# Later GpSimd addends, later sums of h and later scales in a gated linear-attention block loop

## The chip, the cores and the metric

The kernel runs on one core of one Trainium2 chip. The metric is device time in microseconds (us): 1939.26 us is the median of three runs before the change (1938.48 to 1942.68). Engines are named as in the profile: PE is the matrix engine, PEld its weight loads, DVE is VectorE, ACT is ScalarE, POOL is GpSimd, SP is the queue that issues most DMAs.

## The reference, cut to what matters

All arrays are float32. src is 4 x 2048 x 256, there are 16 heads of 64, FF is 1024, and the gate's inner width I is 704.

```python
xn = layernorm(src)
# attention branch
Q, K, v = elu(xn @ Wq + bq) + 1, elu(xn @ Wk + bk) + 1, xn @ Wv + bv
o  = (Q @ (K^T v)) / (Q . sum(K) + 1e-6)          # per head
x1 = layernorm(xn + o @ Wo + bo) * g1 + be1
s  = layernorm(x1 + gelu(x1 @ W1 + b1) @ W2 + b2) * g2 + be2
# gate branch: x and h are rounded to a 4-bit grid in blocks of 16, and so are the weights
h = silu(fp4(xn) @ fp4(w_gate)^T) * (fp4(xn) @ fp4(w_up)^T)
g = silu(fp4(h) @ fp4(w_down)^T)
out = src + s * g
```

## The kernel before, in words

The 8192 rows are worked in 32 blocks of 256 rows (n = 0 to 31), 8 blocks to a batch. K^T v and the sum of K over a whole batch are needed before a block of that batch can be finished. So a first loop makes the keys of batch 0, and in the main loop (line 1041) the 24 blocks of batches 0 to 2 also make the keys of the batch after theirs, in two "subs" per block (each sub is 256 rows by half of the features). The 8 blocks of the last batch (n = 24 to 31) have no keys to make; `subs` is empty there.

A block of the main loop does, in the order of the program:

- `q_of` (741): the product pq, then Q on ACT and DVE, four pieces `zq<-e,q` (767);
- `keys_k` (511) for the first sub: product pk, `k<-pk,bk` (491), exp on ACT, `kk<-ek,k` on DVE (500), and on POOL the running sum `kacc` (502, 504);
- `quantized_x`, `quantized_h` (683, 689): the grid of x and h times its scales, `qT<-qT,gridT`. The scales reach qT by a DMA that spreads them (670), the grid by a transposing DMA (680). `sums` (769): pz, `z<-pz`, `z<-z`, and z goes out to memory and comes back spread as zb by DMAs;
- `gate_up` (694) of the next block: pg, and h by ACT and DVE; `keys_xk` (526): pxk from kk;
- `down` (719): pd, the gate g on ACT, then three POOL operations: `o = g*be2` (735), `o = o + src` (736), `g = g*g2` (737);
- `qz` (796): `zq<-zq,zb`, Q divided by its sum, in two halves on DVE;
- `ffn_sums` (861) for block n-1: four DVE operations `hs` on h^T, for a product with fewer multiplications (seven instead of eight);
- `keys_k` for the second sub; `attention` (802): pa, x1 = xn + pa, statistics, on POOL the power -0.5 (377), normalization; `keys_xk` for the second sub;
- most of `ffn_2(n-1)` (880): py; `scales_h(n+1, j)` for j = 0, 1 (642) and `scales_x(n+2)` (621): reduce, scale, reciprocal on DVE;
- `x1_T` (818): transposes of x1, then on POOL `x1*g1` (830) and `+ shift` (831);
- `grid_of_h`, `grid_of_x` (645, 625): the rounding to the grid, and after it on POOL `xn + bo` (640);
- `output(n-1)` (904): the sum of py and x1 (`s`), its statistics, on POOL the power -0.5, then `o<-s,rstd,o` and the store; `ffn_1(n)` (833): pf and hT.

What sets the order: every product keeps the order of the program on PE (98). DVE and ACT keep it in the first loop; from line 1026 on (`in_order[0] = False`) a scheduler fills them, which takes from the instructions that are ready, by its own estimate of times, the one that comes first in the program. POOL is filled in this way throughout. Each engine then executes its list strictly in order. `tc.issue_after(ins)` makes the instructions traced under it stand behind `ins` in their engine's list; it adds no wait on another engine. Products share four PSUM banks (`mm`), and q1, e and kk have three buffers each, xn, x1, g and o two, the tile x (src, loaded for line 736) one.

Of the kernel before, what the change touches and what calls it, by code (L numbers as in the profile page):

```python
# [12 lines left out]
ALU = mybir.AluOpType  # L13
# [9 lines left out]
def linear_attention_gated_by_fp4_ffn(  # L23
# [34 lines left out]
    nc = tc.nc  # L58
# [305 lines left out]
        yield  # L364


    def stats(x, name, js=range(TB)):

        j0, j1 = js[0], js[-1] + 1
        mv = small.tile([P, TB, 2], F32, tag="mv", name=f"mv_{name}")  # L370
        rstd = small.tile([P, TB], F32, tag="rstd", name=f"rstd_{name}")
        for j in js:
            st = small.tile([P, 6], F32, tag="st", name=f"st_{name}_{j}")
            vector.bn_stats(st, x[:, j, :])
            vector.bn_aggr(mv[:, j, :], st)
        vector.tensor_scalar(rstd[:, j0:j1], mv[:, j0:j1, 1], LN_EPS, None, ALU.add)
        nc.gpsimd.tensor_tensor(rstd[:, j0:j1], rstd[:, j0:j1], neg_half[:, j0:j1], ALU.pow)  # L377
        return mv, rstd

    def normalize(dst, x, mv, rstd):  # L380
# [115 lines left out]
    def key_elu(b, f, k1, e, nm, first):  # L496

        kacc = keys[b, "acc", f]
        kk = work.tile([P, HALF], F32, tag="kk", name=f"kk_{nm}", bufs=3)
        ins = vector.scalar_tensor_tensor(kk, e, 1.0, k1, ALU.min, ALU.max)  # L500
        if first:
            nc.gpsimd.tensor_copy(kacc, kk)
        else:
            nc.gpsimd.tensor_tensor(kacc, kacc, kk, ALU.add)  # L504
        return kk, ins.ins

    def key_xk(b, f, xn, j, kk, first, last):
# [105 lines left out]
    def load_xn(n):  # L613
        blk[n]["xn"] = work.tile([P, TB, D], F32, tag="xn", name=f"xn_{n}", bufs=2)
        nc.sync.dma_start(blk[n]["xn"], xn_d[n])

    def load_xnT(n):
        blk[n]["xnT"] = work.tile([P, ND, T], F32, tag="xnT", name=f"xnT_{n}", bufs=1)
        nc.sync.dma_start(blk[n]["xnT"], xnT_d[n])
# [5 lines left out]
    def grid_of_x(n, issue=None):  # L625
        xn = blk[n]["xn"]
        y = work.tile([P, TB * D // BLK, BLK], F32, tag="y", name=f"y_{n}", bufs=1)
        per_j = D // BLK
        out = [
            (  # L630
                grid_x[:, :, j, :].rearrange("p c (k e) -> p c k e", e=BLK),
                j * per_j, (j + 1) * per_j,
            )
            for j in range(TB)
        ]
        fp4_grid(
            blocks(xn.rearrange("p j d -> p (j d)")), blk[n].pop("rs_x"), y, out, f"x_{n}", issue
        )

        nc.gpsimd.tensor_tensor(xn, xn, rows["bo"], ALU.add)  # L640

    def scales_h(n, j):
        blk[n]["rs_h", j] = fp4_scale(blocks(blk[n]["h"][j]), scale[:, : I // BLK, j], f"h_{n}_{j}")
# [45 lines left out]
    def quantized_h(n, j):  # L689

        qh = qT[:, :NI, j * P : (j + 1) * P]
        return vector.tensor_tensor(qh, qh, gridT[n][:, j * NI : (j + 1) * NI, :], ALU.mult)
# [26 lines left out]
    def down(n, j):  # L719
        if j == 0:  # L720
            blk[n]["pd"] = acc_tile(f"pd_{n}").rearrange("p (j d) -> p j d", j=TB)
        pd = blk[n]["pd"]
        for i in range(NI):
            mm(
                pd[:, j, :], qT[:, i, j * P : (j + 1) * P], wd[:, i, :], start=i == 0, stop=i == NI - 1
            )
        if j < TB - 1:
            return
        g = work.tile([P, TB, D], F32, tag="g", name=f"g_{n}")
        scalar.activation(g, pd, AF.Silu)  # L730

        o = work.tile([P, TB, D], F32, tag="o", name=f"o_{n}")
        x = work.tile([P, TB, D], F32, tag="x", name=f"x_{n}", bufs=1)
        nc.sync.dma_start(x, rows_of(src, n))
        nc.gpsimd.tensor_tensor(o, g, rows["be2"], ALU.mult)  # L735
        nc.gpsimd.tensor_tensor(o, o, x, ALU.add)
        nc.gpsimd.tensor_tensor(g, g, rows["g2"], ALU.mult)
        blk[n]["g"], blk[n]["o"] = g, o


    def q_of(n, first=None):
# [54 lines left out]
    def qz(n):  # L796
        zq, zb = blk[n]["zq"], blk[n].pop("zb")
        for g in range(2):
            cs = slice(4 * g, 4 * g + 4)
            vector.tensor_tensor(zq[:, cs, :], zq[:, cs, :], zb[:, cs, :], ALU.mult)  # L800

    def attention(n):
        zq = blk[n].pop("zq")
# [14 lines left out]
    def x1_T(n):  # L818
        x1 = blk[n]["x1"]
        pt = transposes(x1, f"x1_{n}")  # L820
        x1T = work.tile([P, ND, T], F32, tag="x1T", name=f"x1T_{n}", bufs=1)
        for c in range(ND):
            ins = scalar.activation(
                x1T[:, c, :], pt[:, c, :], AF.Identity,
                bias=cols["be1"][:, c : c + 1], scale=cols["g1"][:, c : c + 1],
            )
        blk[n]["x1T"] = x1T
        blk[n]["act"] = ins.ins

        nc.gpsimd.tensor_tensor(x1, x1, rows["g1"], ALU.mult)  # L830
        nc.gpsimd.tensor_tensor(x1, x1, rows["shift"], ALU.add)

    def ffn_1(n, chunks=range(NF)):
        x1T = blk[n]["x1T"]
# [203 lines left out]


    last = NBLK - 1  # L1040
    for n in range(NBLK):
        b, bi = divmod(n, NB)
        subs = (2 * bi, 2 * bi + 1) if b + 1 < B else ()
        if n < last:
            gate = gate_up(n + 1)
        for sub in subs if n == 0 else ():
            keys_T(b + 1, sub)
        if subs:
            step(m_half)
            q_of(n)  # L1050
            step(down_1)
            load_xnT(n + 1)
            kk_ins = keys_k(b + 1, subs[0])
            with tc.issue_after(kk_ins):
                ins = quantized_x(n)
            with tc.issue_after(sums(n, ins.ins).ins):
                for j in range(TB):
                    quantized_h(n, j)
            if n > 0:
                keys_T(b + 1, subs[1], keys["exp"])  # L1060
            step(m_half)
            keys_xk(b + 1, subs[0])
            step(gate, 9)
            step(m_half)
            down(n, 0)
            down(n, 1)
        elif n < last:
            def values():
                quantized_h(n, 0)
                return quantized_x(n)  # L1070

            step(m_half)
            q_of(n, values)
            quantized_h(n, 1)
            load_xnT(n + 1)
            down(n, 0)
            sums(n)
            step(m_half)
            step(gate, 9)
            step(m_half)  # L1080
            down(n, 1)
        else:
            for j in range(TB):
                quantized_h(n, j)
                down(n, j)
        with tc.issue_after(blk[n + 1]["late"]) if n < last else nullcontext():
            qz(n)
        if not subs:
            ffn_2(n - 1, 4 if n < last else 8)
        if n > 0:  # L1090
            ffn_sums(n - 1)
        if subs:
            keys_k(b + 1, subs[1])
        attention(n)
        if n + 2 < NBLK:
            load_xn(n + 2)
        if subs:
            keys_xk(b + 1, subs[1])
            if subs[1] % NB == NB - 1:
                m_half = m_of_half(b + 1, subs[1] // NB)  # L1100
                step(m_half)
        bn, bin_ = divmod(n + 1, NB)
        next_subs = (2 * bin_, 2 * bin_ + 1) if bn + 1 < B else ()
        for sub in next_subs if n > 0 else ():
            keys_in(bn + 1, sub)
        if n > 0:
            ffn_2(n - 1, 20)
        more = n + 1 < NBLK, n + 2 < NBLK
        if more[0]:
            for j in range(TB):  # L1110
                scales_h(n + 1, j)
            if more[1]:
                scales_x(n + 2)
        for sub in next_subs if n == 0 else ():
            keys_in(bn + 1, sub)
        for sub in next_subs[:1]:
            keys_apart(bn + 1, sub)
        x1_T(n)
        for sub in next_subs[1:]:
            keys_apart(bn + 1, sub, blk[n]["act"])  # L1120

        if n > 0 and not subs:
            ffn_2(n - 1, 26)
        if more[0]:
            spread_scales(n + 1, *more)
        if n > 0:
            ffn_2(n - 1, 28)
        if more[0]:
            grid_of_h(n + 1, 0)
            grid_T(n + 1, 0, NI)  # L1130
            grid_of_h(n + 1, 1, blk[n]["act"])
            if more[1]:
                grid_of_x(n + 2, blk[n]["act"])
            grid_T(n + 1, NI, (NCH if more[1] else NI) * TB)
        if n > 0:
            output(n - 1)
        if n + 1 == last:
            q_of(last)
            ffn_1(n, range(NF // 2))
            sums(last)  # L1140
            ffn_1(n, range(NF // 2, NF))
        else:
            ffn_1(n)
        for sub in next_subs[:1]:
            keys_T(bn + 1, sub, blk[n]["gelu"])
# [38 lines left out]
```

## Time and profile before

| | |
|---|---|
| median of 3 runs | 1939.26 us |
| the profiled execution | 1948.53 us, span 1946.4 us, granted PE clock 0.995 |
| PE busy | 1895.5 us, 97% of the span, 8788 instructions |
| DVE busy | 1440.9 us, 74% |
| ACT busy | 803.7 us, 41% |
| POOL busy | 562.3 us, 29%, 461 instructions |
| mean DMA traffic | 96 GB/s |

POOL's operations that the change moves, each 32 times, by 128 x 512 elements, with the mean time of one:

| line | what | mean ns |
|---|---|---|
| 735 | o = g*be2 | 1567 |
| 736 | o = o + src | 1708 |
| 737 | g = g*g2 | 1867 |
| 830 | x1 = x1*g1 | 1274 |
| 831 | x1 = x1 + shift | 1418 |
| 640 | xn = xn + bo | 1402 |

How to read it: the times of the profile count from the start of the span. A row of the timeline gives the start, the busy time of the instructions that it merges (their number stands at the end, x2), the engine, the line, the operation, out<-in, and in brackets how long the engine was idle before it and what ended that. Nearly all DVE and ACT instructions have line 115, since a helper records them; they are told apart by their tiles. An fp32 product appears as two PE instructions for each one of the program. The end of a PE instruction is modelled: instructions of one kind start 0.216 us apart (128x256, 32 of them in 7.07 us) while each is shown as 0.38 us long.

### The profile page before, as it was taken

The numbers are of one execution on the slowest core, as the hardware profiler recorded it, in microseconds if no ns is written. First come the engines' busy times: TensorE is split into PE (matmuls) and PEld (weight loads), VectorE is DVE, ScalarE is ACT, GpSimd is POOL, SyncE is SP. The second block draws the span as 40 slices with busy tenths as digits, with TensorE's granted clock in tenths as the row PEclk, the third lists the DMA queues.
The fourth block names the chain that finished last, engine by engine and source line by source line (L and its number), as shares of the span: only waits on it lengthen the run. The fifth ranks groups of instructions, "written<-read, shape, count | busy, mean of one in ns | idle before, by whom it ended". The sixth has DMA issues, their size and how long they took to land. (4 is left out here: it accounts for less than half of the span.)

```text
span 1946.4 us, 24467 instructions
## 1 busy us (share of the span) xinstructions
PE 1895.5 (97%) x8788; PEld 1379.9 (71%) x8788; DVE 1440.9 (74%) x2554; ACT 803.7 (41%) x1384; POOL 562.3 (29%) x461
## 2 busy tenths in 40 slices
PE   9989999999999999999999999999999999999997
PEld 4446677667777777777677777776776688788776
DVE  7878577776677777777777778776767778788775
ACT  2334554334444355542344543444433344444342
POOL 4441233322233232332222333222323212222212
PEclk9999999999999999999999999999999999999999
DMA  4435545344444455644343553465442444445441
GB/s 148 146 93 119 114 102 108 101 102 86 87 70 94 113 101 118 134 80 101 84 85 71 118 109 101 97 122 104 84 90 65 71 81 86 82 90 89 76 80 42
DMA packets 225120, 187.11 MB, mean 96 GB/s; under 512 B 103364, under 2 KB 185568, under 8 KB 225000
## 3 DMA queue, kind: packets, MB, share of 16 engines
q1 hardware_dynamic: 224168, 183.99, 44.8%
q10 hardware_dynamic: 832, 1.57, 0.3%
q8 instruction: 69, 1.13, 0.3%
q14 instruction: 51, 0.42, 0.1%
HBM read 131.41 MB, written 31.54 MB: 84 GB/s over the span
## 5 line engine op out<-in xcount | busy, mean ns | idle before, releaser
L99 PE MATMUL pg<-wgu,qT 128*128 128x352 f32 x1024 | 310.4, 461 | 0.1
L99 PEld LDWEIGHTS pg<-wgu,qT 128*128 128x128 f32 x1024 | 193.2, 190 | 118.7 <-issue 14.0
L504 POOL TENSOR_TENSOR kacc<-kacc,kk 128x512 f32<-128x512 f32 x120 | 171.9, 1433 | 339.8 <-DVE kk L115 337.7
L99 PE MATMUL pxk<-kk,xn_k 128*128 128x512 f32 x512 | 237.1, 602 | 19.7 <-DVE kk L115 19.6
L99 PE MATMUL pa<-m,zq 128*128 128x256 f32 x1024 | 229.9, 382 | 8.2 <-DVE zq L115 8.0
L99 PE MATMUL pk<-wk_sb,xnT_k 128*128 128x512 f32 x512 | 232.1, 596 | 1.4 <-ACT xnT_k L115 1.0
L99 PE MATMUL pq<-xnT,wq_sb 128*128 128x256 f32 x1024 | 228.0, 381 | 1.6 <-ACT hT L115 1.6
L99 PEld LDWEIGHTS pa<-m,zq 128*128 128x128 f32 x1024 | 194.5, 191 | 47.6 <-issue 13.0
L99 PE MATMUL pf<-x1T,w_sb 128*128 128x256 f32 x1024 | 226.7, 379 | 0.0
L115 ACT ACT_TABLE_LOAD x122 | 156.5, 1283 | 166.8 <-DVE k L115 153.9
L99 PEld LDWEIGHTS pq<-xnT,wq_sb 128*128 128x128 f32 x1024 | 195.6, 191 | 28.8 <-ACT hT L115 2.0
L735 POOL TENSOR_TENSOR o<-g,be_r 128x512 f32<-128x512 f32 x32 | 50.1, 1567 | 573.5 <-ACT g L115 549.8
L99 PEld LDWEIGHTS pf<-x1T,w_sb 128*128 128x128 f32 x1024 | 192.0, 190 | 25.5 <-issue 0.4
L99 PEld LDWEIGHTS pxk<-kk,xn_k 128*128 128x128 f32 x512 | 91.5, 189 | 129.6 <-issue 78.0
L99 PE MATMUL pd<-wd,qT 128*128 128x256 f32 x768 | 172.4, 379 | 1.7 <-DVE qT L115 1.7
L99 PEld LDWEIGHTS pk<-wk_sb,xnT_k 128*128 128x128 f32 x512 | 97.6, 191 | 104.1 <-issue 97.4
L99 PEld LDWEIGHTS pd<-wd,qT 128*128 128x128 f32 x768 | 145.7, 190 | 26.2 <-DVE qT L115 2.7
L115 DVE SCALAR_TENSOR_TENSOR zq<-e,q 128x512 f32<-128x512 f32 x128 | 86.8, 688 | 104.2 <-ACT e L115 104.2
L377 POOL TENSOR_TENSOR rstd<-rstd,neg_half 128x2 f32<-128x2 f32 x96 | 72.8, 759 | 283.4 <-DVE rstd L115 266.2
L115 ACT ACTIVATE h<-pg 128x352 f32<-128x352 f32 x128 | 58.9, 460 | 191.5 <-PE pg L99 191.5
L115 ACT ACTIVATE ek<-k,neg_one 128x512 f32<-128x512 f32 x128 | 89.7, 719 | 116.3 <-DVE k L115 115.9
L115 DVE SCALAR_TENSOR_TENSOR kk<-ek,k 128x512 f32<-128x512 f32 x128 | 90.2, 713 | 61.6 <-ACT ek L115 61.6
(133 smaller groups left out, 2776.9 us busy)
## 6 DMA issues: line engine op xcount, KB each, us to landing
zb<-z_d SPq DMA_DIRECT2D x128, 256.0 KB
qT<-scale_d SPq DMA_DIRECT2D x248, 128.0 KB
x_k<-in_L_attn_src_dram SPq DMA_DIRECT2D x32, 256.0 KB
x<-in_L_attn_src_dram SPq DMA_DIRECT2D x32, 256.0 KB
xn_d<-xn_k SPq DMA_DIRECT2D x32, 256.0 KB
xn<-xn_d SPq DMA_DIRECT2D x32, 256.0 KB
xnT_d<-xnT_k SPq DMA_DIRECT2D x32, 256.0 KB
xnT<-xnT_d SPq DMA_DIRECT2D x32, 256.0 KB
```

The source lines that it names most:

```text
L99: return tc.keep_in_program_order(nc.tensor.matmul(*args, **kw))
L115: ins = op(*args, **kw)
L377: nc.gpsimd.tensor_tensor(rstd[:, j0:j1], rstd[:, j0:j1], neg_half[:, j0:j1], ALU.pow)
L504: nc.gpsimd.tensor_tensor(kacc, kacc, kk, ALU.add)
L735: nc.gpsimd.tensor_tensor(o, g, rows["be2"], ALU.mult)
```

## The change

Three things move; no operation is added or taken away.

1. POOL's six operations leave the places where their inputs are made. 735 to 737 become `gate_addend(n-1)`, traced at the very start of block n. 830 and 831 become `ffn_addend(n-1)` and 640 becomes `attention_addend(n+1)`; both are called by `block_addends(n)`. In the blocks with keys that stands behind the first `keys_k`, in blocks 24 to 30 behind `q_of`, in block 31 at the start. All are put behind the last POOL operation traced so far (`pool["last"]`): a power of `stats`, a kacc sum, or the addend before.
2. `ffn_sums(n-1)` is put behind the second `kk` of the second keys on DVE, and in blocks 24 to 31 behind the second half of `qz`. The second `keys_k` is traced before it.
3. In blocks without keys `scales_h(n+1, 1)` is put behind the second half of `qz`.

The core of the diff:

```diff
@@ stats
-        nc.gpsimd.tensor_tensor(rstd[:, j0:j1], rstd[:, j0:j1], neg_half[:, j0:j1], ALU.pow)
+        pool["last"] = nc.gpsimd.tensor_tensor(
+            rstd[:, j0:j1], rstd[:, j0:j1], neg_half[:, j0:j1], ALU.pow
+        ).ins
@@ key_elu
+        pool["last"] = acc.ins
@@ new function; grid_of_x loses its last line
+    def attention_addend(n):
+        xn = blk[n]["xn"]
+        with tc.issue_after(pool["last"]):
+            pool["last"] = nc.gpsimd.tensor_tensor(xn, xn, rows["bo"], ALU.add).ins
@@ down loses its three POOL operations, x1_T its two
+    def gate_addend(n):
+        g, o, x = (blk[n][k] for k in ("g", "o", "x"))
+        with tc.issue_after(pool["last"]):
+            nc.gpsimd.tensor_tensor(o, g, rows["be2"], ALU.mult)
+            nc.gpsimd.tensor_tensor(o, o, x, ALU.add)
+            pool["last"] = nc.gpsimd.tensor_tensor(g, g, rows["g2"], ALU.mult).ins
+
+    def ffn_addend(n):
+        x1 = blk[n]["x1"]
+        with tc.issue_after(pool["last"]):
+            nc.gpsimd.tensor_tensor(x1, x1, rows["g1"], ALU.mult)
+            pool["last"] = nc.gpsimd.tensor_tensor(x1, x1, rows["shift"], ALU.add).ins
@@ main loop
+    def block_addends(n):
+        if n > 0:
+            ffn_addend(n - 1)
+        for i in (0, 1) if n == 0 else (n + 1,):
+            if i <= last:
+                attention_addend(i)
+
     for n in range(NBLK):
...
+        if n > 0:
+            gate_addend(n - 1)
         if subs:
             step(m_half)
             q_of(n)
             step(down_1)
             load_xnT(n + 1)
             kk_ins = keys_k(b + 1, subs[0])
+            block_addends(n)
...
             step(m_half)
             q_of(n, values)
+            block_addends(n)
             quantized_h(n, 1)
...
         else:
+            block_addends(n)
             for j in range(TB):
                 quantized_h(n, j)
                 down(n, j)
         with tc.issue_after(blk[n + 1]["late"]) if n < last else nullcontext():
-            qz(n)
+            qz_ins = qz(n)
         if not subs:
             ffn_2(n - 1, 4 if n < last else 8)
+        kk_ins = keys_k(b + 1, subs[1]) if subs else qz_ins
         if n > 0:
-            ffn_sums(n - 1)
-        if subs:
-            keys_k(b + 1, subs[1])
+            with tc.issue_after(kk_ins):
+                ffn_sums(n - 1)
         attention(n)
...
-            for j in range(TB):
-                scales_h(n + 1, j)
+            scales_h(n + 1, 0)
+            with tc.issue_after(qz_ins) if not subs else nullcontext():
+                scales_h(n + 1, 1)
...
+        if n == last:
+            gate_addend(n)
         x1_T(n)
+        if n == last:
+            ffn_addend(n)
```

More of the change, by code (lines that the diff above doesn't have):

```diff
@@ L364, in quantize_down @@
         yield
+    pool = {}
     def stats(x, name, js=range(TB)):
@@ L501, in key_elu @@
         if first:
-            nc.gpsimd.tensor_copy(kacc, kk)
+            acc = nc.gpsimd.tensor_copy(kacc, kk)
         else:
-            nc.gpsimd.tensor_tensor(kacc, kacc, kk, ALU.add)
+            acc = nc.gpsimd.tensor_tensor(kacc, kacc, kk, ALU.add)
+        pool["last"] = acc.ins
         return kk, ins.ins
@@ L638, in grid_of_x @@
         )
-        nc.gpsimd.tensor_tensor(xn, xn, rows["bo"], ALU.add)
     def scales_h(n, j):
@@ L734, in down @@
         nc.sync.dma_start(x, rows_of(src, n))
[L735 to L738, printed above, removed]
+        blk[n]["g"], blk[n]["o"], blk[n]["x"] = g, o, x
+    def gate_addend(n):
[9 more added lines that the diff above has]
+            pool["last"] = nc.gpsimd.tensor_tensor(x1, x1, rows["shift"], ALU.add).ins
     def q_of(n, first=None):
@@ L799, in qz @@
             cs = slice(4 * g, 4 * g + 4)
-            vector.tensor_tensor(zq[:, cs, :], zq[:, cs, :], zb[:, cs, :], ALU.mult)
+            ins = vector.tensor_tensor(zq[:, cs, :], zq[:, cs, :], zb[:, cs, :], ALU.mult)
+        return ins.ins
     def attention(n):
@@ L828, in x1_T @@
         blk[n]["act"] = ins.ins
-        nc.gpsimd.tensor_tensor(x1, x1, rows["g1"], ALU.mult)
-        nc.gpsimd.tensor_tensor(x1, x1, rows["shift"], ALU.add)
     def ffn_1(n, chunks=range(NF)):
```

## The prediction

> **What bounds the kernel now.** The page first: PE is busy for 1895.5 of 1946.4 us, so a change can win only where PE stands still. The view of waits on PE, in two windows, says where. In the main loop up to block 23 (195 to 1600 us):
>
> ```profile
> PE pxk L99 <- DVE kk L115: 14.1, 11, 1.7
> ```
>
> and in the last batch (1600 us to the end):
>
> ```profile
> PE pa L99 <- DVE zq L115: 8.0, 7, 2.8
> PE pd L99 <- DVE qT L115: 1.7, 2, 1.1
> ```
>
> The first is the second keys' kk, which comes late in bi = 3 to 6 of each batch; the second is the second half of Q / sum. An idle time counts from a modelled end, which lies 0.16 us behind the next slot (0.38 - 0.216), so a stall is 0.16 more than its row. Blocks with keys and no stall start 57.1 us apart, which is PE alone: nothing is to be won in them.
>
> Why DVE is late is in the timeline of block 12, DVE and then POOL:
>
> ```profile
> 895.18 0.88 DVE L115 TENSOR_REDUCE scale<-h 128x44 f32<-128x704 f32 x1
> 895.98 3.05 DVE L115 TENSOR_TENSOR hs<-hT 128x512 f32<-128x512 f32 x2
> 898.95 1.25 DVE L115 TENSOR_SCALAR scale<-scale 128x44 f32<-128x44 f32 x1
> ...
> 903.20 1.27 DVE L115 TENSOR_TENSOR k<-pk,bk 128x512 f32<-128x512 f32 x2
> ```
>
> ```profile
> 895.54 1.27 POOL L735 TENSOR_TENSOR o<-g,be_r 128x512 f32<-128x512 f32 x1 [19.02 <-ACT g L115]
> 896.89 1.60 POOL L736 TENSOR_TENSOR o<-o,x 128x512 f32<-128x512 f32 x1
> 898.44 1.72 POOL L737 TENSOR_TENSOR g<-g,g_r 128x512 f32<-128x512 f32 x1
> ```
>
> Two things are to be seen. pk was done at 898.2, yet k waits until 903.2 behind hs and scales. And the two engines take turns: alone, hs takes 0.68 and the 44-wide scale 0.19; begun while POOL's operation runs, 1.75 and 1.25. Over the trace, each DVE operation that reads two operands from SBUF shows it (y<-m_x 1.72 against 0.68, h<-h,rs 1.95 against 0.89), as tensor_scalar on SBUF does; operations with a PSUM operand, reductions, statistics and reciprocals don't. A DVE operation that starts just behind a POOL operation loses 1.08 us (1.76 - 0.68), and POOL's next waits for DVE's in turn. All POOL rows here read SBUF.
>
> The Trainium skill (SBUF — State Buffer, Who interferes with whom) says the second one to start is blocked for the whole of the other. The row says a little less: with 1.21 us of POOL left, hs took 1.76, not 1.89. By the page each meeting below costs 0.13 more, by my estimate some 2 us in all; the sum goes by the row.
>
> **Part 1, blocks 0 to 23.** Second keys before hs: k can start when pk is there (898.2 at the latest), second kk ends 3.5 us after the second k starts, as in the rows (exp's table load 1.28, two exps 1.3, kk), some 902.5. pa ends at 905.1, so pxk doesn't wait. DVE fills the wait with scales and grid, without POOL. Then hs, 4 x 0.62, beside two kacc (2 x 1.08): done by 907.2. The x1 chain behind it may start 1 us late (x<-xn,pa at 907.3 before) but its transposes stand behind pxk 3.5, py 2.6 and 1.9 us of PE. Gain: 14.1 + 11 x 0.16 = 15.9.
>
> The moved POOL work there: 735 to 737 start behind the power of `output` and last 4.6 us (1.35 from start to start, plus the two `o` in between). DVE is idle from `o` to the first zq, 3.00 us in block 11; earlier `o` (no 830, 831, 640 beside y and grid) makes that some 4. At most zq loses 1, and only pz needs all four, later. The other three stand behind kacc, from about 938.9 in block 13:
>
> ```profile
> 938.04 1.75 DVE L115 RECIPROCAL z<-z 128x256 f32<-128x256 f32 x1
> 939.72 1.76 DVE L115 TENSOR_TENSOR qT<-qT,gridT 128x768 f32<-128x768 f32 x2
> 941.61 0.52 DVE L115 TENSOR_TENSOR h<-h,pg 128x352 f32<-128x352 f32 x1
> 943.97 0.52 DVE L115 TENSOR_TENSOR h<-h,pg 128x352 f32<-128x352 f32 x1 [1.84 <-PE pg L99]
> ```
>
> z is past already. The two qT lose 1.5 together, and pd needs them at 948.4. The first h then ends at 943.6; its bank is wanted at 945.0 (pg's third pair, 2.41 us a pair from 938.97). Hidden, with 1.4 to spare; were that gone, each us over it would cost PE one us in up to 24 blocks. SP: x's load no longer waits for 736 of its own block; out goes 1 to 2 us later, and nothing behind it on SP is due before xnT's load, 4 us on. POOL: behind the six stand kacc and a power, both due much later.
>
> **Part 2, scales behind Q / sum, blocks 25 to 30.** The reduce and POOL's first operation no longer stand before or beside the second zq. Five blocks have a stall of 0.62 + 0.16: 3.9. Block 29 has 2.42 + 0.16, of which grid, 1.98 instead of 0.88, and the reduce go; I leave 0.4: 2.2. In block 31 the zq pair takes 4.48 with POOL beside it; without, pa's second half starts at 1912.0 instead of 1913.5: 1.5. Sum 7.6. Behind the later scale stand its reciprocal, h and grid on DVE, and pscale on PE, which wants it at 1745.7 in block 27, where it was done at 1735.7: ten us to spare.
>
> **Part 3, POOL in the last batch: the cost.** Here nothing stands between the six operations: they all start behind the power of `output`, and run into Q. Block 28:
>
> ```profile
> 1755.25 0.88 DVE L115 SCALAR_TENSOR_TENSOR o<-s,rstd,o 128x256 f32<-128x256 f32 x2 [0.59 <-POOL rstd L377]
> 1758.90 1.56 DVE L115 TENSOR_TENSOR qT<-qT,gridT 128x768 f32<-128x768 f32 x2 [2.77 <-DMA qT<-scale_d]
> 1760.38 1.89 DVE L115 SCALAR_TENSOR_TENSOR zq<-e,q 128x512 f32<-128x512 f32 x3
> 1762.18 0.95 DVE L115 TENSOR_TENSOR qT<-qT,gridT 128x768 f32<-128x768 f32 x1
> 1763.05 0.68 DVE L115 SCALAR_TENSOR_TENSOR zq<-e,q 128x512 f32<-128x512 f32 x1
> 1764.46 0.42 DVE L115 TENSOR_SCALAR z<-pz 128x256 f32<-128x256 f32 x1 [0.73 <-PE pz L99]
> ```
>
> From qT's landing to z this is one chain without a gap, PE waits at its end, and all of it reads two operands from SBUF. Counted from the power's end, POOL's six end at about 1.6, 3.3, 4.6, 5.9, 7.3 and 8.6 us (two `o` in between). qT lands 2.8, 4.6, 3.1, 3.7, 3.4 and 5.1 us after that end in blocks 25 to 30. The power itself comes 2.0 us earlier, since y 1.43 becomes 0.69, y<-m_x 1.72 becomes 0.68 and a scale 0.43 becomes 0.18; the last 0.25 also brings qT forward. So the distances become 4.6, 6.4, 4.9, 5.5, 5.2 and 6.9, and what POOL has left costs (rest of the one running, up to 1.08, and 1.08 for each behind it) 3.2, 1.9, 3.1, 2.5, 2.8 and 1.4. Block 24, whose second qT comes late anyway (1576.97): 1.3. Together 16.2, less 6 x 0.25 for the earlier landing, less 1.0 for blocks 25 and 27, where pz has 0.5 to spare: 13.7. Bounds: nothing, if POOL is through in time; 6 x 1.08 = 6.5 a block, 45, if all six meet the chain. I take 13.7, as the starts follow from rows.
>
> Block 31: five operations meet o, o and four zq from 1891.9 on (0.8 earlier by h<-m_h, 1.68 to 0.88). 5 x 1.25 + 0.8 + 4 x 0.6, less 0.5 of overlap, ends at 1900.9; pz wants the last zq at 1897.8: 3.1. At the end `gate_addend` stands right behind the power that x1's two normalizations wait for; the second loses 1.1, on the path. Together 4.2. Elsewhere x1's power has no POOL operation ahead that isn't done.
>
> **Sum:** -15.9 - 7.6 + 13.7 + 4.2 = -5.6. The profiled execution took 1948.5 us (span 1946.4), 9.2 over the median of 1939.3; I take the difference as it is to the median: **1933.7 us**. About 0.2%, 3.9 us, is what a measurement here can tell from no change.
>
> **Rivals.**
> - POOL gets through before qT lands, or the scheduler orders Q otherwise: the last batch costs 4 or less, -5.6 - 13.7 = -19.3, 1920. For it: DVE idles 2.8 to 4.2 us there today. Against: six operations need 8.6.
> - Slower: POOL's turns in Q. If the power doesn't come earlier, the distances stay as they are and six blocks cost 1.5 to 1.8 more each, 24 in all: 1944; with all six in the chain, 1965. It decides from (23.5 - 4.2) / 7 = 2.8 us a block on; I have 2.0. For it: PE waits at the end of that chain today. Against: the y rows.
> - The change doesn't do what it says: the scheduler still puts other work before k, half of the 15.9 stays, 1941.
>
> **Numbers.** Forecast 0.45 (its own range 1925 to 1940), of which 0.28 faster by over 0.2% and 0.17 within. POOL in time 0.25, faster. POOL's turns 0.20, slower. Not done 0.10, of which 0.07 within and 0.03 slower. Faster 0.53, within 0.24, slower 0.23. The range, 1918 to 1948, takes in 1920, 1941 and 1944 and leaves out the dear end, 1965.
>
> **What would show it.** Right: no wait of pxk for kk in blocks 3 to 22, block starts 57.1 apart; no wait of pa for zq in blocks 25 to 30; zq and qT of 1.2 to 1.8 us in blocks 25 to 30, with POOL lines 735 to 640 beside them, and PE waiting at pz for zq by 1 to 3 us. Wrong: zq still 0.69 there (POOL was through), or h<-h,pg holding pg up in blocks 0 to 23.

## The result, and the profile after

The changed kernel takes 1935.87 us (median of 20 runs, 1932.50 to 1938.32) beside 1940.22 us of the kernel before on the same chip (20 runs, 1936.56 to 1943.94). The ratio is 0.9977, 95% interval 0.9971 to 0.9984: 4.4 us faster by the medians, 3.1 to 5.6 by the interval. The forecast was 5.6 faster. Its profiled execution took 1935.41 us (span 1933.6, granted clock 0.996).

The same two views as of the kernel before are the waits of PE in the main loop and in the last batch. After, the longest in the main loop up to 1600 us (columns: engine, waiting product, what it waited for, us in total, times, longest):

```profile
PE pz L99 <- DVE zq L115: 2.3, 3, 1.1
```

and from 1600 us to the end:

```profile
PE pz L99 <- DVE zq L115: 6.4, 9, 1.1
PE pd L99 <- DVE qT L115: 2.6, 2, 1.9
PE pt_x L102 <- DVE x L115: 2.5, 2, 1.5
PE pa L99 <- DVE zq L115: 1.7, 1, 1.7
```

The 14.1 us of pxk for kk are gone, and of the 8.0 us of pa for zq one wait in block 31 is left. In their place stand, in the last batch, pz waiting for zq (before, the view of that batch has no such wait) and, at the very end, the transposes pt_x waiting for x (2.5 us, 0.5 before).

Where the new wait comes from is in block 28 of the changed kernel, DVE first and then POOL (start, busy time, engine, line, operation, tile, number of instructions merged):

```profile
1737.21 2.89 DVE L115 SCALAR_TENSOR_TENSOR o<-s,rstd,o 128x256 f32<-128x256 f32 x2 [0.58 <-POOL rstd L379]
1742.35 2.64 DVE L115 TENSOR_TENSOR qT<-qT,gridT 128x768 f32<-128x768 f32 x2 [2.25 <-issue]
1744.91 2.96 DVE L115 SCALAR_TENSOR_TENSOR zq<-e,q 128x512 f32<-128x512 f32 x3
1747.80 0.94 DVE L115 TENSOR_TENSOR qT<-qT,gridT 128x768 f32<-128x768 f32 x1
```

```profile
1741.19 1.27 POOL L758 TENSOR_TENSOR x<-x,g_r 128x512 f32<-128x512 f32 x1
1742.55 1.89 POOL L759 TENSOR_TENSOR x<-x,shift_r 128x512 f32<-128x512 f32 x1
1744.40 1.72 POOL L625 TENSOR_TENSOR xn<-xn,bo_r 128x512 f32<-128x512 f32 x1
```

Before, the same pair of qT took 1.56 and the three zq 1.89. Now the pair takes 2.64 and the three take 2.96, each some 1.08 more. Taken one by one, it is the second qT, which begins at 1743.23 while 759 runs, and the first zq, which begins while 625 runs, that take 1.76 each instead of 0.68; the first qT, which was running when 759 began, took 0.96, as in a second profile of the kernel before. When POOL is through, at 1746.1, the next qT takes 0.94, as before (0.95). The landing of qT is 5.2 us behind the power (the prediction worked out 5.5), and six POOL operations need 9.0.

The table gives the stages by the starts of PE's instructions in the traces: from the first pa of block 0 to that of block 23, from there to that of block 31, and from there to the last product. "Before, again" is a second profile of the kernel before (below); the changed kernel has two profiles as well. The last column is the timed ratio with its interval, as us of a kernel before of 1940.

| kernel | 0 to 23 | 23 to 31 | 31 to the end | sum against "before, again" | timed |
|---|---|---|---|---|---|
| before | 1348.8 | 367.6 | 26.3 | +6.7 | |
| before, again | 1347.4 | 362.3 | 26.3 | 0 | |
| after | 1331.3 | 371.8 | 29.8 | -3.1 | -4.5 (-5.6 to -3.1) |
| after, again | 1331.3 | 371.2 | 29.9 | -3.6 | |
| order alone | 1334.1 | 361.7 | 26.3 | -13.9 | -14.6 (-17.8 to -11.4) |
| POOL's move alone | 1331.3 | 377.0 | 29.8 | +2.1 | -2.7 (-4.5 to -1.0) |
| after, scales as before | 1331.3 | 373.5 | 28.4 | -2.8 | -2.5 (-4.7 to -0.6) |
| after, last batch's POOL as before | 1331.3 | 361.6 | 26.3 | -16.8 | -18.0 (-21.3 to -14.7) |
| after, three POOL operations behind z | 1331.3 | 360.8 | 29.6 | -14.3 | -18.2 (-21.7 to -14.7) |
| ... and five behind z in block 31 | 1331.3 | 360.0 | 28.6 | -16.1 | -20.0 (-22.5 to -17.3) |
| ... and two behind z in block 31 | 1331.3 | 358.1 | 26.3 | -20.3 | -21.9 (-25.0 to -18.6) |
| after, three more POOL operations | 1331.3 | 407.9 | 28.3 | +31.5 | +29.3 (+26.2 to +32.4) |

What lies ahead of the first pa, from PE's first instruction on, took 190.1 to 193.9 us, and differed by 1.6 between two profiles of one kernel; it is left out of the sums. "Before, again" itself took 1.7 us less than the median of the kernel before on its chip (1940.19 beside 1941.93).

### The profile page after: what moved, and what is told of

Read it like the earlier page. It is cut to its first block, busy times and chain, and to the rows that moved or that the text cites. A ratio compares the mean times of both kernels' runs of the same rounds, so it can differ in the third digit from the quotient of the medians.

```text
span 1933.6 us, 24461 instructions
## 1 busy us (share of the span) xinstructions
PE 1895.5 (98%) x8788; PEld 1380.9 (71%) x8788; DVE 1494.1 (77%) x2554; ACT 803.0 (42%) x1384; POOL 555.0 (29%) x461
## 3 DMA queue, kind: packets, MB, share of 16 engines
q10 hardware_dynamic: 832, 1.57, 0.3%
## 4 chain that ended last, share of the span: by engine, by line
PE 81%; DVE 7%; issue 4%; DMA 3%; ACT 2%; POOL 1%; SPq 1%; DVEq 0%; POOLq 0%; ACTq 0%
PE pg L99 15%; PE pa L99 11%; PE pk L99 10%; PE pxk L99 9%; PE py L99 9%; PE pf L99 8%; PE pq L99 8%; PE pd L99 8%; DMA qT<-scale_d 2%; DVE qT L115 1%; PE pz L99 1%; DVE zq L115 1%; SPq L678 1%; PE pt_x L102 1%; PE pm L99 1%
## 5 line engine op out<-in xcount | busy, mean ns | idle before, releaser
L508 POOL TENSOR_TENSOR kacc<-kacc,kk 128x512 f32<-128x512 f32 x120 | 178.8, 1490 | 587.4 <-DVE kk L115 585.4
L99 PEld LDWEIGHTS pa<-m,zq 128*128 128x128 f32 x1024 | 193.9, 190 | 38.6 <-issue 12.7
L115 DVE SCALAR_TENSOR_TENSOR zq<-e,q 128x512 f32<-128x512 f32 x128 | 97.3, 771 | 69.9 <-ACT e L115 69.8
L115 ACT ACTIVATE x1T<-pt_x,bcol 128x256 f32<-128x256 f32 x64 | 32.6, 560 | 252.4 <-PE pt_x L102 252.4
L115 ACT ACTIVATE hT<-pf,bcol 128x256 f32<-128x256 f32 x256 | 105.9, 471 | 71.6 <-PE pf L99 71.2
```

What stands on the lines that cost most here:

```text
L99: return tc.keep_in_program_order(nc.tensor.matmul(*args, **kw))
L115: ins = op(*args, **kw)
L508: acc = nc.gpsimd.tensor_tensor(kacc, kacc, kk, ALU.add)
```

## The experiments

### The kernel before, once more

> The kernel before, unchanged, for a second profile of it. The first profiled execution took 1948.5 us, some 8 over its median, and by its trace the changed kernel should be 13 us faster where the timed runs give 4.4. Theory P: the first execution had stretches that an ordinary one doesn't have. This one should lie at 1938 to 1943 us, and its trace should say which: if the waits of pxk for kk in blocks 3 to 22 are still 14 us, the extra is elsewhere (1.8 us of slower pace in block 30, 3 us ahead of the first pa) and the key blocks' gain stands at 16 to 17; if those waits are 6 to 9 us, the key blocks gain only 7 to 10 in an ordinary run. Theory Q: the profile itself makes the kernel before slower by 8 us; then this one is at 1946 or more again, with the same waits.

It took 1940.19 us. The longest of its waits of PE up to 1600 us, and then from there on:

```profile
PE pxk L99 <- DVE kk L115: 12.9, 11, 1.7
```

```profile
PE pa L99 <- DVE zq L115: 5.4, 7, 1.5
```

Theory P: the key blocks' waits are nearly the same (12.9 and 14.1), but the last batch is 5.3 us shorter. The execution that the prediction read had one wait of 2.4 at pa in block 29, which here is 0.8, and behind that wait PE ran at half its clock for 3.4 us (0.72 as a mean over 6 us; the rows are in the last section): pa of that block took 11.07 us from its first start to its last, here 7.75. Its wait ahead of pa of block 31 was 2.75 us, here 1.54. So the 9.8 us between the first profiles (+6.7 and -3.1 in the table) are 3.1 to 3.6 when the two of the changed kernel are put beside this one, and the timed 4.4 agrees with that.

### The order alone

```diff
 (the kernel before, with parts 2 and 3 of the change)
+        kk_ins = keys_k(b + 1, subs[1]) if subs else qz_ins
         if n > 0:
-            ffn_sums(n - 1)
-        if subs:
-            keys_k(b + 1, subs[1])
+            with tc.issue_after(kk_ins):
+                ffn_sums(n - 1)
...
+            scales_h(n + 1, 0)
+            with tc.issue_after(qz_ins) if not subs else nullcontext():
+                scales_h(n + 1, 1)
```

> The order alone: the sums of h stand behind the second keys and the later scales behind Q / sum, but POOL's six operations stay where the kernel before has them. Theory T (the prediction's): the order removes the waits of pxk for kk (about 16 us) and those of pa for zq (about 7), and POOL's move only costs (about 14 in blocks 24 to 30, 4 in block 31). So this kernel is faster than the changed one: 1940 - 23 = 1917 us, 1914 to 1922 with what hs and POOL's old turns may give back. Rival A: it is POOL's move that frees VectorE beside the keys, and the order alone leaves VectorE as late as before: 1936 or more, with waits of pxk for kk of several us in blocks 3 to 23. Rival B: the waits seen in the profile do not count in the timed runs: about 1936 as well, but without those waits in its profile.

1927.87 us, ratio 0.9925 (0.9908 to 0.9941). No wait of pxk for kk is left, so rivals A and B fall. It is not 1917, nor within the 1914 to 1922 that were given: the last batch gains only 0.6 us over "before, again", since pa still waits 4.1 us for zq in it, and the key blocks keep 1.7 us of waits at pscale (0.4 before).

### POOL's move alone

```diff
 (the changed kernel, with parts 2 and 3 undone)
-        kk_ins = keys_k(b + 1, subs[1]) if subs else qz_ins
         if n > 0:
-            with tc.issue_after(kk_ins):
-                ffn_sums(n - 1)
+            ffn_sums(n - 1)
+        if subs:
+            keys_k(b + 1, subs[1])
...
-            scales_h(n + 1, 0)
-            with tc.issue_after(qz_ins) if not subs else nullcontext():
-                scales_h(n + 1, 1)
+            for j in range(TB):
+                scales_h(n + 1, j)
```

> POOL's move alone: the six operations stand where the changed kernel has them, but the sums of h come before the second keys again and both scales of h stand as in the kernel before. Theory T: without POOL beside them four hs and a scale are about 3 to 4 us shorter, so most of the waits of pxk for kk go here too (10 to 16 us), but the last batch pays its 14 + 4 and has no gain from the scales: 1940 - 13 + 18 = 1945 us, 1941 to 1950. That separates the two halves of the change: if the order alone is near 1917 and this one near 1945, the keys' gain can be had by either half and the cost comes from POOL's move alone. Rival A (POOL's move is the gain): 1936 or less.

1939.08 us, ratio 0.9986 (0.9977 to 0.9995): below the range of 1941 to 1950 that was given, though the kernel is slower than the order alone, as expected. By its trace it is 2.1 us over "before, again", by the timed runs 2.7 under. The two executions account for nearly all of that: the profiled one lay 2.0 over its median, "before, again" 1.7 under its own, and 0.9 lie ahead of the first pa. The trace has three stretches of 3.41 us at half clock between blocks 23 and 31, where that of the changed kernel has none; they cost up to 1.7 us each and are in the 377.0 of the table. Its key blocks last 1331.3 us, as in the whole change. So the second keys can be freed by either half: by putting them ahead of hs, or by taking POOL's operations away from hs.

### The scales as before

```diff
-            scales_h(n + 1, 0)
-            with tc.issue_after(qz_ins) if not subs else nullcontext():
-                scales_h(n + 1, 1)
+            for j in range(TB):
+                scales_h(n + 1, j)
```

> The changed kernel with both scales of h as in the kernel before. It prices part 2 of the change beside the rest of it. Theory T: the waits of pa for zq come back in part (6 us by the prediction, 2 to 4 by the kernel in which only POOL moves, where POOL's first operation no longer stands beside the second zq): 1939 to 1943 us where the changed kernel is at about 1937. Rival: with POOL gone from there, both halves of Q / sum are done in time, and the scales' place costs nothing: 1936 to 1938.

1938.63 us, ratio 0.9987 (0.9976 to 0.9997), 1.9 us over the changed kernel, with overlapping intervals, and between the two ranges that were given; the time alone doesn't decide. The trace says 1.7 from block 23 to 31 (373.5 against 371.8), with this line where the changed kernel has one wait:

```profile
PE pa L99 <- DVE zq L115: 2.3, 4, 1.5
```

The stalls of PE inside pa in blocks 24 to 30, by its starts, give a table of two by two: 5.5 us with neither half ("before, again"), 3.6 with the scales moved and POOL not (the order alone), 2.4 with POOL moved and the scales not (this kernel, and POOL's move alone), none with both. So theory T holds for pa: the scales' place costs 2.4 us there once POOL has moved.

### The last batch's POOL operations at their old places

```diff
@@ the ends of grid_of_x, down and x1_T; False: without issue_after
+        if n > NBLK - NB:
+            attention_addend(n, False)
...
+        if n >= NBLK - NB - 1:
+            gate_addend(n, False)
...
+        if n >= NBLK - NB - 1:
+            ffn_addend(n, False)
@@ main loop
-        if n > 0:
+        if 0 < n < NBLK - NB:
             gate_addend(n - 1)
             q_of(n, values)
-            block_addends(n)
```

> The changed kernel, but the POOL operations that would fall into blocks 24 to 31 stand at the places of the kernel before. Theory T: PE's waits at pz for zq in blocks 24 to 30 go (about 14 us), those of block 31 and at the end too (about 4), the keys' gain stays: 1936 - 18 = 1918 us, 1915 to 1923, and zq takes 0.69 us again where the second qT lies before it. Rival C: POOL's turns do not set pz's wait (qT's landing does): within 3 us of the changed kernel, 1933 to 1937.

1924.56 us, ratio 0.9907 (0.9890 to 0.9924), 13.6 us under the changed kernel by the ratios and 13.7 by the traces. Rival C falls. 18 were expected; with POOL at its old places 3.8 us of the stalls at pa come back.

### Three of the six behind z

`after_z` is a new tile of one element, and `blk[n]["z"]` keeps z; their definitions are left out here.

```diff
...
             q_of(n, values)
-            block_addends(n)
             quantized_h(n, 1)
             load_xnT(n + 1)
             down(n, 0)
             sums(n)
+            with tc.issue_after(pool["last"]):
+                pool["last"] = nc.gpsimd.tensor_copy(after_z, blk[n]["z"][:1, :1]).ins
+            block_addends(n)
```

> The changed kernel, but in blocks 24 to 30 the three POOL operations on x1 and xn start only behind z (a POOL copy of one element reads z first); the three on o and g stay behind the power of the output. Theory T: the three that stay end 4.6 us after the power, before qT lands (4.6 to 6.9 us after it), so the wait of pz for zq falls from 2 to 3 us a block to its ordinary 0.6 in blocks 25 to 30: 10 to 13 us less than the changed kernel, 1923 to 1926 us. Rival C (qT's landing sets it) or a theory in which the number of POOL operations, not their place, counts: 1933 to 1937.

1924.08 us, ratio 0.9906 (0.9888 to 0.9924), within the range of theory T. Block 28, the last of the three POOL operations that stay ahead of Q, and DVE behind it:

```profile
1736.39 1.45 POOL L753 TENSOR_TENSOR g<-g,g_r 128x512 f32<-128x512 f32 x1
```

```profile
1739.16 1.56 DVE L115 TENSOR_TENSOR qT<-qT,gridT 128x768 f32<-128x768 f32 x2 [2.45 <-issue]
1740.64 1.89 DVE L115 SCALAR_TENSOR_TENSOR zq<-e,q 128x512 f32<-128x512 f32 x3
```

POOL ends at 1737.8, qT starts at 1739.2, and qT and zq take 1.56 and 1.89 again. The same operations in the same number cost nothing where the chain of Q doesn't meet them.

### Three more POOL operations

```diff
             q_of(n, values)
             block_addends(n)
+            xn = blk[n + 1]["xn"]
+            for _ in range(3):
+                with tc.issue_after(pool["last"]):
+                    pool["last"] = nc.gpsimd.tensor_tensor(xn, xn, rows["bo"], ALU.add).ins
```

> A dose: the changed kernel with three more POOL operations of 128 x 512 behind the six in each of blocks 24 to 30 (they add bo to xn of the next block three times more, so the result of blocks 25 to 31 is another). Theory T: each meets one more VectorE operation of Q and costs up to 1.08 us, so the wait of pz for zq grows by about 3 us a block, 19 to 22 us in all: 1956 to 1960 us beside a changed kernel of about 1937. Rival C (what sets the wait is qT's landing, and POOL's operations come beside it): the three fall behind z, 1937 to 1941.

1971.81 us, ratio 1.0151 (1.0135 to 1.0167), 34 us over the changed kernel by the ratios where 19 to 22 were expected. From its first to its last instruction pz takes 21.4 us more than in the changed kernel, summed over blocks 24 to 30 (3.4 in block 28): the dose that theory T gives, 1.0 us for each added operation. The rest is a second cost behind it. In block 28 PE waits three times for zq within some 5 us, 3.7 us in all, and pg behind it is slow (the last two of the three, and pg):

```profile
1774.31 0.95 PE L99 MATMUL pz<-zq,kh 128*32 128x256 f32 x4 [1.05 <-DVE zq L115]
1776.85 1.07 PE L99 MATMUL pz<-zq,kh 128*32 128x256 f32 x4 [1.59 <-DVE zq L115]
1777.84 11.43 PE L99 MATMUL pg<-wgu,qT 128*128 128x352 f32 x32
```

The table by stretches (from and to, length, busy times of PE, PEld, DVE, ACT and POOL, then the granted clock) has half the clock for the first 3.4 us of pg, against 1.00 behind the shorter waits of the changed kernel:

```profile
1777.88:1781.29 3.41, 3.41 (x8) 2.15 (x7) 2.18 (x2) 0.47 (x1) 0.00 (x0) 0.50 0.09 29
```

Pg lasts 11 us more over the last batch. Between blocks 23 and 31 this trace has 14 such stretches of 3.41 us, that of the changed kernel none.

### Block 31, in two ways

Both kernels start from the one with three operations behind z, and at the end put `ffn_addend(31)` ahead of `gate_addend(31)`. The first has all five of block 30 behind z of block 31 (that they leave the start of block 31 is left out here):

```diff
...
             sums(last)
+            with tc.issue_after(pool["last"]):
+                pool["last"] = nc.gpsimd.tensor_copy(after_z, blk[last]["z"][:1, :1]).ins
+            gate_addend(n)
+            block_addends(last)
             ffn_1(n, range(NF // 2, NF))
```

> The kernel with three of POOL's operations behind z, and block 31 mended too: there the five operations on o, g and x1 of block 30 start behind z of block 31, where VectorE is idle for 7 us until zb comes back, and at the end the two on x1 come before the three on o and g, so that none starts right behind the power that the normalizations of x1 wait for. Theory T: the wait of pz for zq in block 31 (3.1 over the ordinary) and the collisions at the end (3.5 us by the trace) go: 4 to 6.5 us less than with the three behind z alone, 1918 to 1920 us where that one gave 1924. Rival D: pa of block 31, or its transposes, are held by something else that is next: less than 2 us gained, 1922 or more.

1922.49 us, ratio 0.9897 (0.9884 to 0.9911): rival D, at first sight. SP's queue and PE in block 31:

```profile
1870.34 0.34 SPq L808 DMA_DIRECT2D z_d<-z  x1
1874.34 0.33 SPq L743 DMA_DIRECT2D x<-in_L_attn_src_dram  x1
1874.79 2.87 SPq L813 DMA_DIRECT2D zb<-z_d  x4
```

```profile
1876.70 1.95 PE L99 MATMUL py<-w_sb,hT 128*128 128x128 f32 x16
1883.31 9.87 PE L99 MATMUL pa<-m,zq 128*128 128x256 f32 x32 [4.66 <-DVE zq L115]
```

The load of x waits until POOL has read the single tile x (752 ends at 1874.3), and zb's load stands behind it: it is issued 4.45 us after z's store, 1.78 in the changed kernel. PE waits 4.66 us and then takes 9.87 us for a pa of 7.5, since its clock is at 0.50 from 1882.00 to 1888.83.

The second kernel leaves the three of `gate_addend(30)` ahead of Q, as in the blocks before:

```diff
+            gate_addend(n)
             q_of(last)
...
-            gate_addend(n)
             block_addends(last)
```

> The kernel with three operations behind z, block 31 done in the way of the blocks before it: the three on o and g of block 30 right behind the power, only the two on x1 behind z of block 31, and at the end x1's two ahead of the three on o and g. In the kernel with all five behind that z the load of x (src) waited on SP for POOL's second operation, which stood behind z, and the load of zb stood behind it in SP's queue: zb came 2.9 us later, PE waited 4.7 us for it at pa, and ran pa at a granted clock of 0.72 after that, 2.4 us longer. Theory T: without that wait pa's wait is 1.5 to 1.7 again and pa takes 7.1 us, so this kernel is 4 to 6 us faster than that one: 1916 to 1919 us beside a kernel before of 1942, ratio 0.987 to 0.988. Rival D (block 31 has another bound behind it, the transposes or the half of zb that comes last): 1921 to 1924, ratio 0.989 to 0.991.

1919.43 us, ratio 0.9887 (0.9871 to 0.9904), 0.4 us above the range of theory T and below that of rival D. The signs that theory T named are there, or nearly: PE waits 1.41 us ahead of pa of block 31 (1.5 to 1.7 were given) and takes 7.4 us for it (7.1). By the trace it is 4.2 us under the first of the two; the timed intervals overlap. In the last batch its waits of PE at pa and pz are down to these:

```profile
PE pa L99 <- DVE zq L115: 1.6, 2, 1.4
PE pz L99 <- DVE zq L115: 0.6, 1, 0.6
```

It is the fastest kernel of this study by its median, 0.9910 of the changed one by the two ratios (0.9892 to 0.9928 by their two intervals).

### The changed kernel, once more

> The changed kernel once more, for a second profile beside the second one of the kernel before. If the accounts of the traces are right, the stages last the same again: 1331 us from the first pa to that of block 23, 371 to 373 from there to that of block 31; the end is 29.8 us if the granted clock falls behind the late transposes there, 28.3 if it does not. 1932 to 1938 us in all. If the stages differ by more than 2 us from the first profile, the accounts hold only to that width.

1936.47 us; 1331.3, 371.2 and 29.9 us. The accounts hold to 0.6 us.

## Why the prediction was right, and where its terms were not

The forecast of 5.6 us less was right within 1.2 us, and the signs that the prediction named came: no wait of pxk for kk, none of pa for zq in blocks 25 to 30, and PE waiting at pz beside longer qT and zq. Its terms, against "before, again":

- **Part 1, -15.9: measured -16.1.** hs beside two kacc loses 2 x 1.08 as worked out (3.43 us for two, 1.36 alone), and nobody waits for it. But the step gave this gain to the order alone. POOL's move alone gives it too, and what one half does the other can't do again.
- **POOL's move in blocks 0 to 23, nothing: measured nothing.** No wait of pg or pd appears, and pa of the blocks with keys starts 57.1 us apart, but for each fourth (61.4).
- **Part 2, -7.6: mis-sized.** The stalls at pa in blocks 24 to 30 fell by 5.5 us, and only some 2 of these are the scales' (1.9 or 2.4 by the table of two by two); the rest goes with POOL's first operation. The term of 2.2 for block 29 was read from a wait that only that execution had; the ordinary stall there is 1.1. The 1.5 of block 31 never came: pa waits 1.7 and 1.4 us there, 1.5 before, since z is 3.1 us later and zb with it. The two terms of block 31 stood beside each other in the sum without being put in one chain.
- **Part 3, +13.7: measured 13.7.** The time from the first to the last instruction of pz in blocks 24 to 30 was 2.12, 0.69, 1.34, 0.86, 1.18, 0.76 and 1.34 us, and is 4.00, 2.92, 2.41, 2.92, 2.92, 2.92 and 1.34: 1.9, 2.2, 1.1, 2.1, 1.7, 2.2 and 0, 11.1 in all, where 1.3, 2.4, 1.6, 2.4, 2.2, 2.6 and 1.2 were worked out. The other 2.6 are waits just ahead of pz: 1.4 for the first zq and 1.2 ahead of pd. That the totals agree to 0.1 is in part chance: single blocks are off by up to 1.2, and those waits ahead of pz had no term of their own.
- **Block 31, +3.1: measured 3.1** (3.80 against 0.69).
- **The end, +1.1: measured 3.5.** This is the term that was too small. The normalizations of x1 and the transposes behind them, at the end of the changed kernel, and the granted clock by stretches (the column behind POOL's):

```profile
1905.34 2.68 DVE L115 TENSOR_SCALAR x<-x,mv,rstd 128x256 f32<-128x256 f32 x2 [0.17 <-POOL rstd L379]
```

  The same pair in "before, again":

```profile
1913.39 0.73 DVE L115 TENSOR_SCALAR x<-x,mv,rstd 128x256 f32<-128x256 f32 x2 [0.23 <-POOL rstd L377]
```

  The transposes and the clock, at the end of the changed kernel again:

```profile
1906.74 0.33 PE L102 MATMUL pt_x<-ident,x 128*128 128x128 f32 x1 [1.47 <-DVE x L115]
1908.08 0.55 PE L102 MATMUL pt_x<-ident,x 128*128 128x128 f32 x3 [1.01 <-DVE x L115]
1908.47 2.77 PE L99 MATMUL py<-w_sb,hs 128*128 128x128 f32 x16
```

```profile
1905.99:1909.40 3.41, 1.65 (x13) 1.46 (x14) 2.50 (x3) 0.73 (x2) 3.33 (x4) 1.00 0.00 0
1909.40:1912.81 3.41, 3.41 (x15) 3.05 (x14) 1.44 (x4) 1.57 (x2) 2.25 (x2) 0.50 0.00 0
```

  Both normalizations meet POOL, not only the second: 2.68 us for two that took 0.73. PE waits 2.48 us instead of 0.54, which makes 1.9. Then py and pf run at half the clock for 3.41 us, which makes 1.6 more: no step of the prediction had that.
- **Not counted: -1.9.** Small waits of PE ahead of pscale (1.5) and inside pt_x (0.5) in the last batch went away, and the wait ahead of pa of block 31 is 0.2 longer.

From block 23 to 31 that is 11.1 + 2.6 + 3.1 - 5.5 - 1.9 = +9.4 (table: +9.5), and with -16.1 and +3.5 the sum is -3.2, beside a timed -4.4 (-5.6 to -3.1). Of the rivals, "POOL in time", 1920, is near what the kernels with operations behind z give (1924 and 1919). "Not done" is refuted by the waits of pxk, and "POOL's turns dearer" would have needed a power that comes no earlier; qT landed 5.2 us behind it.

Two things were lucky. Part 2 promised some 2 us too much and the end cost 2.4 more than worked out, and the 1.9 that nobody had counted took back part of that. And the prediction made its sum against an execution 9 us over the median and carried the difference to the median as it was. That was sound for the key blocks, whose waits hardly differ between the two profiles of before, and wrong by 1.1 us for block 29.

## What to carry to other kernels

Work that is off the critical path has a price by its place: the same six POOL operations cost nothing beside a DVE that waits, and 1.0 to 1.08 us for each two-operand DVE operation that they meet in a chain at whose end PE waits. Place such work by the end of that chain (here: behind z), and in the last blocks, where there are other neighbours, place it anew. Ask of every operation that is moved what frees its buffers, and which load in a queue waits for that. Before a stall of one profile is counted as a gain, see whether it stands in a second profile.

## What was not expected of the hardware

- A DVE operation with two operands in SBUF that began beside a POOL operation took some 1.08 us more: the second qT and the first zq here (1.76 against 0.68 us each, with 1.21 us of POOL's operation left). The normalizations at the end, half as wide, lost 0.93 and 1.01. The other way round POOL waited: 759, begun while the first qT ran, took 1.89 us, and 1.27 in the kernel with three operations behind z. Adding three POOL operations cost PE 1.0 us each, and POOL's three took 4.93 us where the same three alone, behind z, take 3.8.
- Short waits lower the clock, and they do it in steps. From the first pa to the last product the granted clock of every trace here is 1.00 or 0.50, and what is at 0.50 lasts 3.41 us or a multiple of it. Such a step costs up to 1.7 us. Within one execution the steps lie on one grid: in the changed kernel two of them begin at 151.54 and 1909.40 us, 515 times 3.413 us apart. What differs is how long PE was busy from one line of the grid to the next. At the end of the changed kernel the waits of 1.47 and 1.01 us fall for the most part between 1905.99 and 1909.40, where PE is busy for 1.65 us (rows above), and the next step is at 0.50. The kernel with the scales as before has the same two waits at its end, but there a line of the grid (its lowered steps begin at 8.56 and 1930.26 us, 563 steps apart) parts them, PE is busy for 1.94 and 2.40 us, and the clock stays at 1.00; from block 31 on that kernel takes 28.4 us, the changed one 29.8:

```profile
1906.37:1909.78 3.41, 1.94 (x18) 1.75 (x16) 3.21 (x8) 0.00 (x0) 2.17 (x3) 1.00 0.00 0
1909.78:1913.19 3.41, 2.40 (x21) 2.21 (x22) 1.63 (x2) 1.58 (x3) 3.41 (x3) 1.00 0.00 0
```

  In the first execution of the kernel before, one wait of 2.42 us in block 29 left PE 1.42 us of work in a step, and the next, from 1828.28 on, is at 0.50:

```profile
1824.87:1828.28 3.41, 1.42 (x7) 1.26 (x8) 3.41 (x4) 0.00 (x0) 3.07 (x2) 1.00 0.60 133
```

  A sharp limit these traces don't give: the changed kernel has a step with 1.57 us of work, from 1834.31 on, and 1.00 behind it.
- The Trainium skill (TensorE: Matmul & The Clock Gate, Part 1: The HAM clock gate (the "warmup" mystery)) tells of a free-running window of about 3.4 us, after which an idle array drops to half its clock. The length of the steps, their grid and the 0.50 agree with that; that a step with 1.42 or 1.65 us of work in it was enough is less than the page gives, and here the measurement decides.
